# Who frees a stream buffer: TensorE's matmul in place of ScalarE's copy, four buffers of six blocks for three of five, and 12 row buffers for 16

## The chip, the cores and the metric

The kernel runs on one core of a Trainium2 chip. A core has five engines that run side by side and meet at semaphores: TensorE (PE in the profile; its weight loads are listed apart as PEld), VectorE (DVE), ScalarE (ACT), GpSimd (POOL) and SyncE (SP), which here does nothing but issue transfers. Sixteen DMA engines carry the transfers between HBM and the on-chip memory SBUF. SP's queue and GpSimd's queue of transfers are each worked off in order: a transfer whose condition is not met holds up those behind it. The metric is the device time of one execution in microseconds (us).

## The reference

A graph layer: every node's 128 features are normalized and clipped at zero, every edge sends its source's row through the 128 x 128 matrix of the edge's type, and every node adds up what arrives.

```python
h = jnp.maximum(_layernorm(x, axis=-1), 0.0)       # x: 12500 x 128
xs = h[src]                                         # 200000 edges
for i in range(4):                                  # edge types
    msgs = msgs + jnp.where((edge_type == i)[:, None], xs @ W[i] + b[i], 0.0)
out = x + segment_sum(msgs, dst, num_segments=12500)
```

The edges come sorted by `dst`, and `dst` is drawn as 12500 u^2 with u uniform, so that the first nodes get very many edges and the last few.

## The kernel before

**The table (the first 112 us).** Nodes are loaded in spans of three blocks (`load_span`, 33 spans; block j holds node 98 p + j on partition p). VectorE takes the statistics (L440), ScalarE normalizes (L461), and each value is split into three bf16 terms, which are stored to `htab` in HBM (L506, `third_part`), 768 bytes a node. The loaded spans lie in buffers of the pool `rows`, which has 16 buffers of 1536 bytes a partition. VectorE prepares in the same time the slots of the dense part. Here a planner that simulates the engines sets the order of all instructions.

**Two ways for the edges.** The 200000 edges are cut in 1563 chunks of 128. The first 512 chunks go to only 1392 nodes and are treated as dense; the other 1051 are gathered, in 64 groups of 16 chunks and four small ones at the end. The first three groups fetch rows of `x`; the other 1003 chunks fetch rows of `htab`.

- *Gathered part.* `gather` (L538) has GpSimd fetch a chunk's 128 source rows by an indirect transfer (L544), two chunks to a buffer `hm` of the same pool `rows`. While a group is worked on, the next one's gathers are in the program, and GpSimd issues them as buffers become free. `sum_up` (L569) multiplies each chunk with its one-hot matrix (L578, three matmuls a chunk), ScalarE copies the result (L581), `weigh` applies the four matrices (L605), and VectorE adds into a ring of destination columns (L666), which is turned and put out with `x` every 512 nodes (`leave`, `put_out`, L691, L696, L698; `fetch` loads the `x` rows at L677).

- *Dense part.* Its nodes are worked on in 18 batches of 27 units of three nodes (the first has 17). `count` (L940) makes for each unit the number of edges from every node and type, as a product of one-hots (VectorE makes them at L959 to L967, TensorE multiplies at L985, ScalarE copies the sum into `counts` at L991). `multiply` (L1024) then multiplies the counts with the whole table: for each of the 98 blocks, three matmuls (L1040) whose weights are the block's three terms and whose moving side is the batch's counts (324 columns), all added in one bank of PSUM.

**The stream.** The table does not stay in SBUF; each batch reads it anew. `hsp` is the pool of stream buffers `hs`; a buffer takes `HB` blocks, and SP loads it (L1032). There are `STREAM` = 3 buffers of `HB` = 5 blocks, so a batch has 20 refills (19 of five blocks, one of three). A refill has to wait until the buffer's former blocks have been read. The pool would make it wait for the last matmul that read them. But `held_by` adds a wait for the first of ScalarE's copies of counts (L991) that stands in the program behind that matmul (the list `left_at` holds the copies with the number of stream blocks read before them, `by_blocks`); this wait takes in the other. Only where no such copy stands there does a refill wait for TensorE itself.

**The order.** From the fourth group on the order on TensorE, VectorE and ScalarE is written out by hand: `dense_work` deals the steps of one batch's `multiply` and of the next one's `count` by their columns, `multiply` 0.15 of its length behind (`BEHIND`), so that a batch begins with some counting alone and ends with some multiplying alone; `pace` spreads this work evenly over the groups. SP and GpSimd follow the planner's order.

Of the kernel before, what the change touches and what calls it, by code (L numbers as in the profile page):

```python
# [55 lines left out]
C0 = 512  # L56
UB = 27
MANY = 16
HB = 5
SLOTS = 4  # L60
SETS = 4
STREAM = 3
BEHIND = 0.15
RING = 2048
OT = 4
# [9 lines left out]
def kernel(  # L75
# [10 lines left out]
    nc = tc.nc  # L86
    N, D = x.shape
    E = src.shape[0]
    NT, _, DO = w.shape
# [141 lines left out]
    flag = const.tile([P, 1], I32, name="flag")  # L231

    mid = ExitStack()
    hpool = mid.enter_context(tc.tile_pool(name="rows", bufs=16))
    opool = mid.enter_context(tc.tile_pool(name="onehots", bufs=2))
    spool = mid.enter_context(tc.tile_pool(name="typed", bufs=2))
    x_ps = mid.enter_context(tc.tile_pool(name="x_ps", bufs=4, space=PSUM))
# [279 lines left out]
    def held_by(one, by, reason):  # L517
        tc.add_manual_dep(
            one.ins,
            by.name,  # L520
            mybir.DependencyInfo(mybir.DependencyClass.Sync, mybir.DependencyReason.DATA),
            reason=reason,
        )
# [409 lines left out]
            nc.scalar.copy(acc[:, a:z], pn[:, : z - a])  # L933


    left_at = []
    by_blocks = [0]
    released = []

    def count(vs, counts):  # L940
        todo = []
        sets = []
        for i, u in enumerate(vs):
            of = slots_of(u)
            of = [(i, c, by, n == 0, n == len(of) - 1) for n, (c, by) in enumerate(of)]
            todo += of
            for one in [of[n : n + SLOTS] for n in range(0, len(of), SLOTS)]:
                if not sets or len(sets[-1]) + len(one) > SLOTS:
                    sets.append([])
                sets[-1] += one  # L950
        before = len(released)
        released.extend(None for _ in sets)

        def make(n):
            at = before + n
            o1 = op1.tile([P, SLOTS, P], BF16, name="o1")
            o2 = o2s[:, at % SETS]
            for k, (i, s, by, first, last) in enumerate(sets[n]):
                one = nc.vector.tensor_scalar(o2[:, k, :NB], iota_n, hkT[:, s : s + 1], None, ALU.is_equal)  # L959
                if k == 0 and at >= SETS:  # L960
                    held_by(one, released[at - SETS], "a set of slots has been counted as a whole")
                if by == 1.0:
                    one = nc.vector.tensor_scalar(o1[:, k], iota_1, loT[:, s : s + 1], None, ALU.is_equal)
                else:
                    if by is None:
                        by = byT[:, (s - PAIRS) // 2 : (s - PAIRS) // 2 + 1]
                    one = nc.vector.tensor_scalar(o1[:, k], iota_1, loT[:, s : s + 1], by, ALU.is_equal, ALU.mult)  # L967
                yield o1[:, k], o2[:, k], one.ins

        making = []  # L970
        made = []
        done = 0
        for n, of in enumerate(sets):
            while len(making) < min(n + 3, len(sets)):
                making.append(make(len(making)))
                made.append([])
            for m in range(n, min(n + 2, len(sets))):
                made[m] += list(making[m])
            for k, (i, s, by, first, last) in enumerate(of):
                if n + 2 < len(sets) and len(made[n + 2]) < len(sets[n + 2]):  # L980
                    made[n + 2].append(next(making[n + 2]))
                o1, o2, _ = made[n][k]
                if first:
                    pb = x_ps.tile([P, NB + NT], F32, name="pt")
                one = nc.tensor.matmul(pb, o1, o2, start=first, stop=last)  # L985
                if k == 0:
                    held_by(one, made[n][-1][2], "a set of slots is counted when all of it is made")
                if k == len(of) - 1:
                    released[before + n] = one.ins
                if last:  # L990
                    one = nc.scalar.copy(counts[:, :, i * NT : (i + 1) * NT], pb.rearrange("p (b t) -> p b t", t=NT))  # L991
                    left_at.append((by_blocks[0], one.ins))
                done += 1
                yield done / len(todo)
            made[n] = None

        def check_sums():
            n = len(vs)
            bi = sdp.tile([P, UB], I32, name="bi")
            nc.vector.tensor_copy(bi[:, :n], counts[:, NW, : n * NT].rearrange("p (i t) -> p i t", t=NT)[:, :, 0])  # L1000
            yield True
            bb = sdp.tile([P, 3, UB], I32, name="bb")
            nc.vector.tensor_single_scalar(bb[:, 0, :n], bi[:, :n], 255, op=ALU.bitwise_and)
            nc.vector.tensor_single_scalar(bb[:, 2, :n], bi[:, :n], 16, op=ALU.arith_shift_right)
            yield True
            nc.vector.tensor_single_scalar(bi[:, :n], bi[:, :n], 8, op=ALU.arith_shift_right)
            nc.vector.tensor_single_scalar(bb[:, 1, :n], bi[:, :n], 255, op=ALU.bitwise_and)
            yield True
            bf = sdp.tile([P, 3, UB], F32, name="bf")
            nc.vector.tensor_copy(bf[:, :, :n], bb[:, :, :n])  # L1010
            yield True
            top = sdp.tile([P, 2], F32, name="top")
            nc.vector.tensor_reduce(top[:, 0:1], bf[:, :, :n], AX.XY, ALU.max)
            nc.vector.tensor_reduce(top[:, 1:2], bf[:, :, :n], AX.XY, ALU.add)
            yield True
            nc.vector.tensor_max(most, most, top[:, 0:1])
            nc.vector.tensor_add(held, held, top[:, 1:2])

        checks.append(check_sums())
# [4 lines left out]
    def multiply(vs, counts):  # L1024
        nu = len(vs)

        counts = counts.bitcast(F8)
        pa = a_ps.tile([P, 512], F32, name="pa")
        for j0 in range(0, NW, HB):
            j1 = min(j0 + HB, NW)  # L1030
            hs = hsp.tile([P, HB, D3], BF16, name="hs")
            one = nc.sync.dma_start(hs[:, : j1 - j0, :], htab.rearrange("(p j) f -> p j f", j=NW)[:, j0:j1, :])  # L1032
            free = [by for n, by in left_at if n > by_blocks[0] - STREAM]
            if free and by_blocks[0] >= STREAM:
                held_by(one, free[0], "the buffer of the stream is free")
            del left_at[: len(left_at) - len(free)]
            for j in range(j0, j1):
                of = counts[:, j, : nu * NT * 4].rearrange("p (v m) -> p m v", m=4)[:, :3, :]
                for c in range(3):
                    nc.tensor.matmul(  # L1040
                        pa[:, : 3 * nu * NT].rearrange("p (m v) -> p m v", m=3),
                        hs[:, j - j0, c * D : (c + 1) * D],
                        of,
                        start=(j == 0 and c == 0),
                        stop=(j == NW - 1 and c == 2),
                    )
                if j + 1 == j1:
                    by_blocks[0] += 1
                if j + 1 < NW:
                    yield (j + 1) / NW  # L1050
        sd = sdp.tile([P, 3 * UB * NT], F32, name="sd")
        nc.scalar.activation(sd[:, : 3 * nu * NT], pa[:, : 3 * nu * NT], AF.Copy, scale=512.0)  # L1052
        def tail():
            py = x_ps.tile([P, 3 * UB], F32, name="pt")
            for t in range(NT):
                nc.tensor.matmul(  # L1056
                    py[:, : 3 * nu],
                    wsb[:, t, :],
                    sd[:, : 3 * nu * NT].rearrange("p (v t) -> p v t", t=NT)[:, :, t],
                    start=(t == 0),  # L1060
                    stop=(t == NT - 1),
                )

            def rest():
                for m in range(3):
                    i = 0
                    while i < nu:
                        if vs[i][m] is None:
                            i += 1
                            continue  # L1070
                        k, d = vs[i][m]
                        by = 2 if m < 2 and k == 0 and d >= PAIRS else 1
                        n = next((e for e in range(1, nu - i) if vs[i + e][m] != (k, d + e * by)), nu - i)
                        to = acc[:, d : d + (n - 1) * by + 1 : by]
                        nc.vector.tensor_tensor(to, to, py[:, m * nu + i : m * nu + i + n], ALU.add)
                        i += n

            tails.append(rest)

        tails.append(tail)  # L1080
        yield 1.0
# [448 lines left out]
```

## Time and profile before

| what | us |
|---|---|
| median of three runs | 1751.6 (1746.14 to 1752.2) |
| profiled execution, its own time | 1744.29 |
| its span, first to last instruction | 1742.5 |
| TensorE busy | 1435.4 |
| GpSimd busy | 1031.1 |
| VectorE busy | 1015.9 |
| ScalarE busy | 450.0 |
| mean granted TensorE clock | 0.926 |

The lines below come from that one execution. In a row of the waits stand the engine and line that waited, what ended the wait, the total in us, how often, and the longest. A group of instructions reads: line, engine, operation, tiles out<-in, shapes, count, then busy us and mean ns, then idle us of the engine before them and what ended it. "SPq" is SP's queue of transfers, "DMA hs<-htab" the landing of a refill, "issue" an idle time for which the profile shows no cause, "remote" one whose releaser is not in the trace. In a window's row stand, behind the stretch and its length, each engine's busy us with its count of instructions, the granted clock of TensorE (1.00 is full speed), the busy share of the DMA engines and GB/s. Some matmul records are missing from such a trace, and ends of matmuls are modelled.

### The profile page before, as it was taken

How to read it: one execution, taken by the hardware profiler on the slowest of the kernel's cores; microseconds unless marked ns; L12 is line 12 of the kernel's file. 1: busy time of each engine (PE TensorE's matmuls, PEld its weight loads, DVE VectorE, ACT ScalarE, POOL GpSimd, SP SyncE). 2: the span in 40 equal slices, each digit the busy share in tenths (PEclk: the TensorE clock that was granted, in tenths of full speed). 3: DMA queues.
4: the chain of work that ended last, by engine and by line, in shares of the span. 5: the costliest groups of instructions: out<-in, count | busy, mean ns of one | idle time of the engine just before them, and what ended most of it. 6: DMA issues, size and time to landing. Idle time of an engine off the chain costs nothing.

```text
span 1742.5 us, 32539 instructions
## 1 busy us (share of the span) xinstructions
PE 1435.4 (82%) x10984; PEld 938.3 (54%) x10984; DVE 1015.9 (58%) x5305; ACT 450.0 (26%) x1095; POOL 1031.1 (59%) x1078
## 2 busy tenths in 40 slices
PE   3876779787979787888888889888888989889875
PEld 1345565554656455555555555555555556555554
DVE  6972867565565556574647555756564556555334
ACT  5783322121212121212121222222222222122011
POOL 6536656565656565656665656666656566656561
PEclk8976799998999899999999999999999899999997
DMA  6542466565646465666555555655555655556652
GB/s 204 179 146 81 144 196 188 173 208 169 196 158 206 158 197 169 206 187 193 175 188 189 175 183 174 200 181 187 178 190 169 197 173 189 173 179 188 196 185 67
DMA packets 144538, 308.92 MB, mean 177 GB/s; under 512 B 26762, under 2 KB 77372, under 8 KB 144365
## 3 DMA queue, kind: packets, MB, share of 16 engines
q1 hardware_dynamic: 94685, 204.98, 35.9%
q0 software_dynamic: 49680, 101.81, 19.9%
q8 instruction: 86, 1.41, 0.3%
q14 instruction: 87, 0.71, 0.1%
HBM read 290.65 MB, written 16.04 MB: 176 GB/s over the span
## 4 chain that ended last, share of the span: by engine, by line
PE 52%; issue 19%; DMA 14%; DVE 5%; another core or an unknown queue 4%; ACT 4%; SPq 2%; DVEq 0%; ACTq 0%
PE pa L1040 27%; DMA hs<-htab 14%; PE pt L985 8%; PE py L605 5%; PE ps L578 4%; ACT counts L991 2%; PE pt L1056 2%; SPq L1032 1%; PE ps L635 1%; DVE oh L561 1%; PE py L596 1%; PE pt L691 1%; DVE o L967 1%; ACT sb L581 1%
## 5 line engine op out<-in xcount | busy, mean ns | idle before, releaser
L544 POOL DMA_INDIRECT hm<-htab,srcT x1003 | 974.6, 972 | 642.5 <-issue 227.1
L1040 PE MATMUL pa<-counts,hs 128*128 128x324 fp8e4 (+1 forms) x5292 | 970.4, 309 | 195.1 <-DMA hs<-htab 150.7
L1040 PEld LDWEIGHTS <-hs 128*128 128x128 bf16 x5292 | 490.9, 98 | 478.1 <-DMA hs<-htab 187.3
L959 DVE TENSOR_SCALAR o<-iota_n,hkT 128x392 bf16<-128x392 f16 x1167 | 381.3, 327 | 97.7 <-PE pt L985 44.1
L985 PE MATMUL pt<-o,o 128*128 128x396 bf16 x1167 | 374.9, 345 | 23.2 <-issue 10.4
L991 ACT CAST counts<-pt 128x396 int32<-128x396 f32 x476 | 230.0, 493 | 555.8 <-PE pt L985 306.3
L561 DVE TENSOR_SCALAR oh<-iota_b,keyT 128x56 bf16<-128x56 bf16 (+8 forms) x1003 | 171.5, 258 | 328.9 <-PE py L596 89.8
L581 ACT COPY sb<-ps 128x224 f32<-128x224 f32 (+8 forms) x251 | 99.7, 397 | 529.4 <-PE ps L578 237.5
L666 DVE TENSOR_TENSOR ring<-ring,py 128x14 f32 (+7 forms) x976 | 171.2, 175 | 82.5 <-PE py L605 20.8
L578 PEld LDWEIGHTS <-hm 128*128 128x128 bf16 x3009 | 166.1, 100 | 75.3 <-issue 30.1
L578 PE MATMUL ps<-oh,hm 128*128 128x56 bf16 (+8 forms) x3009 | 189.3, 199 | 18.0 <-issue 13.9
L967 DVE TENSOR_SCALAR o<-iota,loT 128x128 bf16<-128x128 bf16 x644 | 175.2, 272 | 0.0
L985 PEld LDWEIGHTS <-o 128*128 128x128 bf16 x1167 | 114.0, 99 | 77.3 <-issue 23.9
L967 DVE TENSOR_SCALAR o<-iota,loT,byT 128x128 bf16<-128x128 bf16 x417 | 139.6, 335 | 0.0
L605 PE MATMUL py<-sb,wsb 128*128 128x224 f32 (+7 forms) x488 | 130.3, 410 | 0.4 <-issue 0.3
L605 PEld LDWEIGHTS py<-sb,wsb 128*128 128x128 f32 x488 | 89.9, 197 | 24.6 <-issue 2.2
L528 POOL DMA_INDIRECT hx<-in_x_dram,srcT x48 | 50.9, 1060 | 34.1 <-issue 12.1
L1000 DVE COPY bi<-counts 128x27 int32<-128x27 int32 (+1 forms) x18 | 4.2, 232 | 106.0 <-issue 62.0
L600 ACT CAST cnt<-py 128x224 bf16<-128x224 f32 (+7 forms) x61 | 24.1, 395 | 112.4 <-PE py L596 35.2
L461 ACT ACTIVATE h<-hm,nmrt,rstdt 128x128 f32<-128x128 f32 x98 | 42.7, 492 | 2.2 <-DVE vart L446 1.9
L1056 PEld LDWEIGHTS pt<-sd,wsb 128*128 128x128 f32 x144 | 31.3, 304 | 6.9 <-ACT sd L1052 4.8
L1056 PE MATMUL pt<-sd,wsb 128*128 128x81 f32 (+1 forms) x144 | 31.0, 379 | 4.7 <-ACT sd L1052 4.7
(234 smaller groups left out, 639.6 us busy)
## 6 DMA issues: line engine op xcount, KB each, us to landing
hs<-htab SPq DMA_DIRECT2D x342, 480.0 KB
hm<-htab,srcT POOLq DMA_INDIRECT x1003
htab<-h SPq DMA_DIRECT2D x32, 288.0 KB
xo<-in_x_dram SPq DMA_DIRECT2D x23, 256.0 KB
out_dram<-xo SPq DMA_DIRECT2D x23, 256.0 KB
hs<-htab SPq DMA_DIRECT2D x18, 288.0 KB
hm<-in_x_dram SPq DMA_DIRECT2D x18, 192.0 KB
hm<-in_x_dram SPq DMA_DIRECT2D x14, 168.0 KB
```

The lines of the kernel that those rows point to most:

```text
L544: one = nc.gpsimd.indirect_dma_start(out=hm[:, (i - h0) * D3 : (i - h0 + 1) * D3], out_offset=None, in_=htab, in_offset=bass.IndirectOffse ...
L561: nc.vector.tensor_scalar(oh[:, i, :], iota_b[:, :K], keyf[:, at : at + 1], None, ALU.is_equal)
L578: nc.tensor.matmul(ps[:, i - i0, :], rows(i, c), oh[:, i, :], start=(c == 0), stop=(c == 2))
L581: nc.scalar.copy(sb[:, i0:i1].rearrange("p g t n -> p g (t n)"), ps[:, : i1 - i0, :])
L605: nc.tensor.matmul(py[:, :g, :], wsb[:, t, :], sb[:, :g, t, :], start=False, stop=(t == NT - 1))
L666: nc.vector.tensor_tensor(to, to, of(i), ALU.add)
L959: one = nc.vector.tensor_scalar(o2[:, k, :NB], iota_n, hkT[:, s : s + 1], None, ALU.is_equal)
L967: one = nc.vector.tensor_scalar(o1[:, k], iota_1, loT[:, s : s + 1], by, ALU.is_equal, ALU.mult)
L985: one = nc.tensor.matmul(pb, o1, o2, start=first, stop=last)
L991: one = nc.scalar.copy(counts[:, :, i * NT : (i + 1) * NT], pb.rearrange("p (b t) -> p b t", t=NT))
L1040: nc.tensor.matmul(pa[:, : 3 * nu * NT].rearrange("p (m v) -> p m v", m=3), hs[:, j - j0, c * D : (c + 1) * D], of, start=(j == 0 and c == 0),
L1056: nc.tensor.matmul(py[:, : 3 * nu], wsb[:, t, :], sd[:, : 3 * nu * NT].rearrange("p (v t) -> p v t", t=NT)[:, :, t], start=(t == 0), stop= ...
```

## The change

The list of ScalarE's copies and the extra wait on them are taken out: a refill of a stream buffer waits for the matmul that read the buffer last, and for nothing of ScalarE's. The stream gets four buffers of six blocks for three of five: a batch has 17 refills (16 of six blocks, one of two), each of 576 KB where it was 480 KB. The pool `rows`, from which both the loads of nodes and the gathered rows take their buffers, has 12 for 16. Per partition the stream grows from 11520 to 18432 bytes and the rows shrink from 24576 to 18432.

In the order as built, TensorE's matmuls, VectorE's one-hots and ScalarE's copies of the long stage stand as they did. In the first 112 us the planner gives another order on all engines but GpSimd, since loads of nodes wait for earlier buffers: load 12 is the first to wait for one, where load 16 was.

```diff
-HB = 5
+HB = 6
-STREAM = 3
+STREAM = 4
...
-    hpool = mid.enter_context(tc.tile_pool(name="rows", bufs=16))
+    hpool = mid.enter_context(tc.tile_pool(name="rows", bufs=12))
...
-    left_at = []
-    by_blocks = [0]
     released = []
...
                 if last:
-                    one = nc.scalar.copy(counts[:, :, i * NT : (i + 1) * NT], pb.rearrange("p (b t) -> p b t", t=NT))
-                    left_at.append((by_blocks[0], one.ins))
+                    nc.scalar.copy(counts[:, :, i * NT : (i + 1) * NT], pb.rearrange("p (b t) -> p b t", t=NT))
...
             hs = hsp.tile([P, HB, D3], BF16, name="hs")
-            one = nc.sync.dma_start(hs[:, : j1 - j0, :], htab.rearrange("(p j) f -> p j f", j=NW)[:, j0:j1, :])
-            free = [by for n, by in left_at if n > by_blocks[0] - STREAM]
-            if free and by_blocks[0] >= STREAM:
-                held_by(one, free[0], "the buffer of the stream is free")
-            del left_at[: len(left_at) - len(free)]
+            nc.sync.dma_start(hs[:, : j1 - j0, :], htab.rearrange("(p j) f -> p j f", j=NW)[:, j0:j1, :])
             for j in range(j0, j1):
...
-                if j + 1 == j1:
-                    by_blocks[0] += 1
                 if j + 1 < NW:
                     yield (j + 1) / NW
```

## The prediction

> **What bounds the kernel now.** I read the page's totals first, then the table of waits for the whole span, then the chain of waits around one of the stalls, then the timeline and short windows there.
>
> ```profile
> span 1742.5 us, 32539 instructions
> PE 1435.4 (82%) x10984; PEld 938.3 (54%) x10984; DVE 1015.9 (58%) x5305; ACT 450.0 (26%) x1095; POOL 1031.1 (59%) x1078
> ...
> L1040 PE MATMUL pa<-counts,hs 128*128 128x324 fp8e4 (+1 forms) x5292 | 970.4, 309 | 195.1 <-DMA hs<-htab 150.7
> ```
>
> ```profile
> SPq L1032 <- ACT counts L991: 633.3, 146, 12.1
> ```
>
> ```profile
> PEld L1040 <- DMA hs<-htab: 187.3, 106, 8.5
> PE pa L1040 <- DMA hs<-htab: 150.7, 88, 8.1
> ```
>
> TensorE is the busiest engine, and what it waits for in the long stage is one thing: the stream buffer `hs`. The queue of SP, which issues these transfers, stands 633 us in front of ScalarE's copies of counts. So the buffers are refilled late, and late because of the copy, not because of the transfer. One place shows it, in the chain (start, length, what):
>
> ```profile
> 822.39 0.32 SPq L1032
> 822.71 0.05 issue
> 822.76 0.02 SPq L1032
> 822.78 10.68 issue
> 833.45 3.34 DMA hs<-htab
> 836.80 0.05 issue
> 836.84 0.99 PE pa L1040 x3
> ```
>
> and in the timeline of the same stretch:
>
> ```profile
> 827.01 1.45 PE L1040 MATMUL pa<-counts,hs 128*128 128x324 fp8e4 x9
> ...
> 832.94 0.49 ACT L991 CAST counts<-pt 128x396 int32<-128x396 f32 x1 [0.16 <-remote]
> ...
> 836.84 0.99 PE L1040 MATMUL pa<-counts,hs 128*128 128x324 fp8e4 x3 [5.06 <-DMA hs<-htab]
> ```
>
> TensorE had read the last of the batch's buffers by 828.5. The next refill goes out at 833.45, when the first copy of the next batch's counts ends; it lands 3.34 us later, and TensorE has stood 5.06 us. This turn comes once per batch (18 batches); the other stalls are shorter ones of the same kind.
>
> The stall has a second price:
>
> ```profile
> core 0: us, PE busy (x) PEld busy (x) DVE busy (x) ACT busy (x) POOL busy (x), PEclk, DMA share, GB/s
> 190.00:1690.00 1500.00, 1278.01 (x10221) 845.74 (x10220) 869.01 (x4610) 330.51 (x786) 913.85 (x941) 0.95 0.58 185
> ...
> 829.60:833.00 3.40, 1.59 (x9) 0.48 (x8) 2.27 (x13) 0.78 (x3) 2.33 (x3) 1.00 0.28 79
> 833.00:836.40 3.40, 0.00 (x0) 0.00 (x0) 1.61 (x9) 0.43 (x1) 2.48 (x4) 0.50 0.70 207
> 836.40:839.90 3.50, 3.06 (x13) 2.27 (x14) 0.00 (x0) 0.00 (x0) 0.69 (x1) 0.51 0.84 332
> 839.90:843.30 3.40, 3.40 (x36) 2.27 (x36) 2.60 (x14) 1.04 (x3) 1.79 (x2) 1.00 0.12 32
> ```
>
> After a stretch of 3.4 us with TensorE 47% busy the granted clock halves, and it comes back only after a busy stretch: 13 matmuls in 3.5 us, then 36 in 3.4. Over the long stage the mean grant is 0.95.
>
> **The change part by part.**
>
> *Release by TensorE, four buffers of six.* A refill now waits for the last matmul that read its buffer. Between that matmul and the first that needs the refill stand three other buffers, 3 x 6 blocks x 3 = 54 matmuls, or 42 where one of them is the short buffer of two blocks that ends a batch.
>
> ```profile
> 783.36 0.59 PE L1040 MATMUL pa<-counts,hs 128*128 128x324 fp8e4 x3
> 783.80 0.33 PE L985 MATMUL pt<-o,o 128*128 128x396 bf16 x1
> 783.96 0.59 PE L1040 MATMUL pa<-counts,hs 128*128 128x324 fp8e4 x3
> ...
> 784.17 0.49 ACT L991 CAST counts<-pt 128x396 int32<-128x396 f32 x1
> ```
>
> ```profile
> hs<-htab SPq DMA_DIRECT2D x342, 480.0 KB
> ```
>
> Three of these matmuls take 783.80 - 783.36 = 0.44 us, so 54 take 8 us and 42 take 6.2 us, with no slot or row work between. Landing took 3.34 us for 480 KB; for 576 KB I estimate 3.34 x 1.2 = 4.0. Both spacings cover it, so I let all these stalls go. What they are worth: 150.7 us by the matmuls' row, 187.3 by the weight loads'. The loads' row starts while the last matmul still runs, one spacing of 0.15 us in each of 106 waits: 187.3 - 16 = 171 us. Taken: 171; the ends are kept. The refills drop from 20 to 17 a batch (98 blocks), with the same bytes.
>
> Queued behind SP's waits are not only refills:
>
> ```profile
> SPq L698 <- DVE xo L696: 41.8, 12, 9.5
> ```
>
> A refill behind such a wait is late by up to 9.5 us against 8 - 4 = 4 us to spare; the mean of 3.5 us is hidden, the longest would show some 5 us. Bound 0 to +10, in the 8 us below.
>
> *The clock.* A grant of 0.95 means (1 - 0.95) x 2 = 10% of 1500 us, 150 us, at half speed. TensorE is busy 85% of the stage, so up to 128 us of work runs at half speed and 64 us could come back; 0 is the other end. Of its 1500 - 1278 = 222 us idle the stream is 171, 77%; I take 77% of 64 = 49 us.
>
> The Trainium skill ("TensorE: Matmul & The Clock Gate", Part 1) says that an idle window of about 3.4 us halves the clock and a busy one restores it. The window above halved it with 47% busy, so this trace does not agree: it shows more loss than the rule says. By the rule as written that stall would have cost no clock, and the forecast would be the first rival's 1588.
>
> *TensorE's signals.* At most 306 buffers end in a matmul that has to signal SP. The matmul of 783.80 releases the copy of 784.17, and the next starts 0.16 us after it, no later than the 396 columns need: 0 us, and 0.03 us a signal would still be +9 us, the upper bound. The Trainium skill (same page, Part 3, "The cost: per-tile semaphore tail") puts 26 ns on each signal; that would be 306 x 0.026 = 8 us on top.
>
> *Rows, 12 buffers for 16.* A buffer holds two gathered chunks, so GpSimd runs 24 chunks ahead, not 32.
>
> ```profile
> L544 POOL DMA_INDIRECT hm<-htab,srcT x928 | 901.6, 972 | 579.5 <-issue 209.7 <-PE ps L578 186.7 <-PE pt L985 96.0
> ```
>
> ```profile
> POOL hm L544 <- issue: 212.2, 687, 0.6
> POOL hm L544 <- PE ps L578: 190.2, 107, 6.8
> ```
>
> A gather costs 0.97 us and 212.2 / 687 = 0.31 us before it, 1.28 us; a group of 16 takes 20.5 us. The rest of its idle time is waiting for buffers, that is, for TensorE. The stage of 1500 us has some 61 groups, 24.6 us each; with 171 + 49 us gone it is 21.0. GpSimd then has 0.5 us a group to spare where it had 4. With 24 chunks of lead, 31 us, a landing like the stream's 3 to 4 us hides. TensorE has no wait for `hm` among its waits today; I take 0, with 0 to +20 us if the margin fails in places.
>
> *The first 112 us.* The same pool takes the loads of nodes.
>
> ```profile
> L192 SPq DMA_DIRECT2D hm<-in_x_dram x15: 13/246/555, 26.8 to 76.2; - x15
> ```
>
> ```profile
> L440 DVE BATCH_NORM_STATS2 stt<-hm x98: 233/276/295, 5.0 to 88.2; 128x6 f32<-128x128 f32 x98
> L461 ACT ACTIVATE h<-hm,nmrt,rstdt x98: 477/492/519, 13.9 to 108.1; 128x128 f32<-128x128 f32 x98
> ```
>
> Load number u now waits for span u - 12, not u - 16, to be normalized. Normalizing goes at (108.1 - 13.9) / 33 = 2.9 us a span, so span 20 is done at about 13.9 + 21 x 2.9 = 75 us, and the last load (32) went out at 76.2, twelve before its statistics at 88.2. SP's stores of the table stand behind these waits, and the planner reorders VectorE's work here. Bound -6 to +6 (half of those twelve either way); 0 taken.
>
> *What is late next.* VectorE's one-hots:
>
> ```profile
> PE pt L985 <- DVE o L967: 7.6, 3, 4.1
> ```
>
> With TensorE not waiting elsewhere VectorE has less time to run ahead; as much again, +8 us, is charged for this and for SP's other waits together.
>
> *The end.* The last gather starts 33 us before the span's end:
>
> ```profile
> L544 POOL DMA_INDIRECT hm<-htab,srcT x1003: 941/949/2188, 114.2 to 1709.7; - x168
> ```
>
> The last 27 chunks need 27 x 1.28 = 35 us of GpSimd, and 24 may be ahead: 0, at most +5.
>
> **Sum.** The profiled execution took 1744.3 us (span 1742.5). 1744.3 - 171 - 49 + 8 = 1532. The median of the runs, 1751.6, stands 7 us above this execution, so 1539 is forecast for a median: 12% less.
>
> **Rivals.**
>
> *The half-speed stretches stay*, because other gaps halve the clock: 1744.3 - 171 + 8 + 7 = 1588. Against it: the window of 829.6 that led into one.
>
> *The gathers become the bound.*
>
> ```profile
> L578 PE MATMUL ps<-oh,hm x3009: 179/197/294, 149.8 to 1729.2; 128*128 128x56 bf16 x27, 128*128 128x80 bf16 x27, 128*128 128x48 bf16 x24, 128*128 128x64 bf16 x24
> ```
>
> 150 us lie before their use and 33 after the last; 24 of the 1003 are there by then, and 979 follow one another. At 1.28 us that is 150 + 1253 + 33 = 1436 us; it decides from (1532 - 183) / 979 = 1.38 us a gather. In the stage they now come every 1500 / 941 = 1.59 us, waits included. Halfway, 1.44: 183 + 1410 + 7 = 1600. For it: a margin of 0.5 us a group. Against: nothing in the trace slows a gather but TensorE.
>
> *The change does not do what it says*: the refills still go out late, held by SP's other waits, and a quarter of the gain comes: 1744.3 - 55 + 7 = 1696. Against: 41.8 us of such waits against 633.
>
> *Slower*: with 12 buffers TensorE comes to wait for its rows. Release, gather, landing and use is a ring of 24 chunks; it binds when one trip takes more than 24 x 1.59 = 38 us, against a landing of some 4 us and two gathers of 1.28. To lose by 0.5% it would have to eat the 212 + 9 us as well, 1.59 + 221 / 979 = 1.82 us a chunk, a trip of 44 us: 1761 or more. Nothing in the profile points there.
>
> **How the numbers follow.** Forecast 0.62 (own range 1500 to 1570: ends of the stall term, 64 us of clock, +20). Half-speed stays 0.15 and gathers bind 0.12, near 1588 and 1600, both reaching 1625. A quarter only 0.05; no change within 0.5% (9 us, about what a measurement of this kernel tells from none) 0.02; slower 0.04. Faster: 0.62 + 0.15 + 0.12 + 0.05 = 0.94. The lower end is 1744.3 - 187 - 64 - 6 + 7 = 1494, taken as 1490; to hold eight in ten with some over, the upper end takes in both of these: 1625.
>
> **What would show it.** Right: SP's wait for the copies gone and its wait for TensorE in its place, with the stream's row in TensorE's waits under 20 us; granted clock 0.98 or more in the long stage; GpSimd's wait for buffers down from 0.3 to some 0.05 us a gather. Wrong: a wait of TensorE for `hm`, or long gaps before L985 ended by VectorE, or refills that go out right after another DMA of SP's.

## The result, and the profile after

The changed kernel takes 1665.6 us in the median of four runs (1663.0 to 1668.0); the kernel before, run beside it, 1751.9 us. The ratio is 0.950 with a 95% interval of 0.945 to 0.955: a gain of 86 us, where 212 were forecast. 1665.6 lies outside the range of 1490 to 1625.

The stream's stall is gone all the same. From the page of the changed kernel (the stream's matmul is L1033 now, its refill L1029):

```profile
span 1661.2 us, 32454 instructions
PE 1417.4 (85%) x10984; PEld 921.7 (55%) x10984; DVE 1014.6 (61%) x5305; ACT 446.9 (27%) x1095; POOL 1030.6 (62%) x1078
...
L544 POOL DMA_INDIRECT hm<-htab,srcT x1003 | 975.0, 972 | 565.5 <-issue 230.9
L1033 PE MATMUL pa<-counts,hs 128*128 128x324 fp8e4 (+1 forms) x5292 | 963.3, 305 | 79.2 <-issue 69.7
```

and from its waits, the largest of SP's queue:

```profile
SPq L1029 <- PE ps L578: 371.9, 88, 10.1
SPq L1029 <- PE pt L983: 312.8, 79, 8.5
```

SP's queue no longer stands in front of ScalarE's copies (633.3 us before) but of TensorE, and no wait of TensorE for `hs` is left (150.7 us before). The clock is better too; in the stretch of the long stage:

```profile
190.00:1610.00 1420.00, 1260.59 (x10164) 826.53 (x10162) 860.09 (x4560) 325.87 (x781) 911.28 (x937) 0.98 0.61 194
```

The grant is 0.98 where it was 0.95. But TensorE is busy 1260.59 of 1420 us, 89% (85% before), and what it waits for now has no name:

```profile
PE pa L1033 <- issue: 69.7, 134, 3.8
PE ps L578 <- issue: 32.7, 56, 1.2
```

One such place, in the timeline of TensorE, then of ScalarE, then of GpSimd (start, length, what; in brackets the idle time before it):

```profile
776.56 0.34 PE L578 MATMUL ps<-oh,hm 128*128 128x64 bf16 x6
776.74 1.72 PE L1033 MATMUL pa<-counts,hs 128*128 128x324 fp8e4 x9
...
779.34 0.28 PE L578 MATMUL ps<-oh,hm 128*128 128x64 bf16 x4
780.07 0.23 PE L578 MATMUL ps<-oh,hm 128*128 128x64 bf16 x2 [0.45 <-issue]
...
783.12 0.59 PE L1033 MATMUL pa<-counts,hs 128*128 128x324 fp8e4 x3 [0.89 <-ACT sd L1043]
```

```profile
776.26 0.37 ACT L581 COPY sb<-ps 128x256 f32<-128x256 f32 x1 [4.56 <-remote]
782.36 0.37 ACT L581 COPY sb<-ps 128x256 f32<-128x256 f32 x1 [5.73 <-PE pt L983]
```

```profile
776.50 1.01 POOL L544 DMA_INDIRECT hm<-htab,srcT  x1 [1.23 <-remote]
777.81 1.24 POOL L544 DMA_INDIRECT hm<-htab,srcT  x1 [0.30 <-issue]
779.35 1.17 POOL L544 DMA_INDIRECT hm<-htab,srcT  x1 [0.30 <-issue]
780.83 0.95 POOL L544 DMA_INDIRECT hm<-htab,srcT  x1 [0.30 <-issue]
782.59 0.94 POOL L544 DMA_INDIRECT hm<-htab,srcT  x1 [0.82 <-PE pt L983]
```

Three things are to be seen. TensorE stops for 0.45 us between the fourth and the fifth of six matmuls on one buffer, where it can have nothing to wait for. The six matmuls at 776.56 end a bank of four chunks, and ScalarE, idle, copies that bank at 782.36, 5.5 us after their record ends. And GpSimd issues four gathers 1.3 to 1.5 us apart, then stands 0.8 us (1.2 us before the first of them) until TensorE's signal comes, within 0.25 us of the start of ScalarE's copy. Counted over the stage from 230 to 1590 us, the copy of four chunks starts 3.35 us in the middle after the record of their last matmul begins (2.13 us in the kernel before, by the same count). TensorE's semaphore updates come in bunches: about half, some 660 of 1297, fall in the some 120 us in which GpSimd has been idle for more than 0.75 us; in such a bunch they follow each other by 0.08 us in the middle, though the matmuls that gave them lie further apart.

By place, with the groups counted from 0, so that group 3 is the first that fetches rows of `htab`: from the start of group 5 to that of group 62 a group takes 24.25 us (25.51 before, 21.0 forecast), 71.5 us less over 57 groups. Group 5 begins 13.6 us earlier, group 3 0.5 later; from group 62 on the kernel takes 3.8 us longer. Together 81.3 us, the difference of the two spans.

### The profile page after: what moved, and what is told of

It reads as the page before. It is cut to its first block, busy times and chain, and to the rows that moved or that the text cites. A ratio compares the mean times of both kernels' runs of the same rounds, so it can differ in the third digit from the quotient of the medians.

```text
span 1661.2 us, 32454 instructions
## 1 busy us (share of the span) xinstructions
PE 1417.4 (85%) x10984; PEld 921.7 (55%) x10984; DVE 1014.6 (61%) x5305; ACT 446.9 (27%) x1095; POOL 1030.6 (62%) x1078
## 4 chain that ended last, share of the span: by engine, by line
PE 74%; DVE 11%; issue 9%; another core or an unknown queue 2%; ACT 1%; DMA 1%; POOL 0%; SPq 0%; DVEq 0%; ACTq 0%; POOLq 0%
PE pa L1033 43%; PE pt L983 11%; PE ps L578 6%; PE py L605 6%; DVE o L957 2%; DVE o L965 2%; PE pt L1047 1%; DVE ring L666 1%; DVE oh L561 1%; PE ps L635 1%; PE py L596 1%; PE pt L691 1%; DVE stt L440 1%; POOL hm L544 0%
## 5 line engine op out<-in xcount | busy, mean ns | idle before, releaser
L544 POOL DMA_INDIRECT hm<-htab,srcT x1003 | 975.0, 972 | 565.5 <-issue 230.9
L1033 PE MATMUL pa<-counts,hs 128*128 128x324 fp8e4 (+1 forms) x5292 | 963.3, 305 | 79.2 <-issue 69.7
L1033 PEld LDWEIGHTS <-hs 128*128 128x128 bf16 x5292 | 492.3, 97 | 353.9 <-issue 132.7
L983 PE MATMUL pt<-o,o 128*128 128x396 bf16 x1167 | 369.5, 337 | 40.3 <-DVE o L965 21.4
L965 DVE TENSOR_SCALAR o<-iota,loT 128x128 bf16<-128x128 bf16 x644 | 177.2, 275 | 0.0
L983 PEld LDWEIGHTS <-o 128*128 128x128 bf16 x1167 | 111.3, 98 | 98.9 <-issue 30.2
L965 DVE TENSOR_SCALAR o<-iota,loT,byT 128x128 bf16<-128x128 bf16 x417 | 142.0, 340 | 0.0
L605 PEld LDWEIGHTS py<-sb,wsb 128*128 128x128 f32 x488 | 86.4, 190 | 32.9 <-issue 11.7
L490 PE MATMUL ps<-h,ident 128*128 128x384 f32 (+1 forms) x34 | 17.2, 591 | 15.7 <-issue 11.4
L596 PE MATMUL py<-oh,three 128*32 128x224 bf16 (+7 forms) x244 | 21.2, 311 | 7.6 <-issue 3.9
```

Source lines behind the costliest of these rows:

```text
L544: one = nc.gpsimd.indirect_dma_start(out=hm[:, (i - h0) * D3 : (i - h0 + 1) * D3], out_offset=None, in_=htab, in_offset=bass.IndirectOffse ...
L605: nc.tensor.matmul(py[:, :g, :], wsb[:, t, :], sb[:, :g, t, :], start=False, stop=(t == NT - 1))
L1033: nc.tensor.matmul(pa[:, : 3 * nu * NT].rearrange("p (m v) -> p m v", m=3), hs[:, j - j0, c * D : (c + 1) * D], of, start=(j == 0 and c == 0),
```

## Experiments

The theory formed from this trace: while GpSimd issues gathers, TensorE's signals leave late ("held signals"); consumers and GpSimd itself wait, TensorE's queue fills (its records never run more than some 31 matmuls ahead of a signal that is still out), and the groups take the length of GpSimd's cycle. The rivals: TensorE's own work is longer than the spacing of its records tells; the traffic holds it up; GpSimd's lead of 24 chunks is too short. The kernels ran on several chips, each beside the kernel before on the same chip, and ratios are to that; between chips the ratios are compared, since the kernel before does not take the same time on each.

**No gathers.** Same bytes, buffers and waits:

```diff
-                one = nc.gpsimd.indirect_dma_start(out=hm[...], in_=htab, in_offset=...)
+                j = (t0 + i) % (N // P)
+                one = nc.sync.dma_start(hm[:, (i - h0) * D3 : (i - h0 + 1) * D3], htab[j * P : (j + 1) * P, :])
```

> Built from the changed kernel (1665.6 us). Each of the 1003 gathers of 128 rows of htab by GpSimd is replaced by a plain transfer of 128 consecutive rows of htab on SP's queue: the same bytes into the same 12 buffers, the same waits, but GpSimd makes no descriptors in the long stage; the gathered part of the result is not the reference's. Three theories for the gain that is missing (24.2 us a group of 16 chunks where 21.0 was forecast). Held signals: while GpSimd issues gathers, TensorE's signals leave late (the copy of four finished chunks starts 3.3 us in the middle after its last matmul's record), TensorE's queue of some 31 matmuls fills and it stops at places where it has nothing to wait for; without the gathers the groups fall to about 21 us, 59 groups x 3.1 = 180 us less, about 1480 us. TensorE's own work: the matmuls take longer than the spacing of their records tells, the records run ahead and the pauses are that queue; no change, 1650 to 1680. Traffic: 186 GB/s of transfers hold up the reading of weights; the bytes are the same, so no change, 1650 to 1680. A buffer lead of 12 that is too short would also leave it at 1650 to 1680.

Measured: 1425.4 us, 0.815 of the kernel before (0.812 to 0.818), 240 us under the changed kernel. On its page:

```profile
L1029 PE MATMUL pa<-counts,hs 128*128 128x324 fp8e4 (+1 forms) x5292 | 927.1, 301 | 0.5 <-ACT sd L1039 0.5
L1029 PEld LDWEIGHTS <-hs 128*128 128x128 bf16 x5292 | 490.8, 96 | 230.1 <-issue 0.7
```

The same 5292 matmuls have 0.5 us of idle time before them for 79.2, the groups take 20.56 us, and a copy follows its last matmul's start by 0.24 us. Traffic is higher (217 GB/s over the span for 186). So TensorE's own work, traffic and lead fall as the cause; what is left is something that comes with GpSimd's gathers.

**More and fewer signals of TensorE.** Three sizes of the same stream room, and rows in larger buffers:

```diff
-HB = 6            # eight_of_three: 3        three_of_eight: 8
-STREAM = 4        # eight_of_three: 8        three_of_eight: 3
```

```diff
+HR = 4            # four_rows: gathered rows in 6 buffers of four chunks
-    hpool = mid.enter_context(tc.tile_pool(name="rows", bufs=12))
+    hpool = mid.enter_context(tc.tile_pool(name="rows", bufs=6))
```

> The changed kernel with the stream in eight buffers of three blocks instead of four of six: the same bytes and the same room, but TensorE signals 594 freed stream buffers instead of 306 and SP issues twice as many refills of half the size. Held signals: each signal of TensorE has a price while GpSimd gathers; spread over all, 0.8 us lost per four chunks over about 6.9 signals is 0.12 us each, 284 more signals are +33 us, about 1700; if a signal costs as much as the 0.72 us in which queued signals are seen to follow each other, up to +200. TensorE's own work and traffic: no change, 1655 to 1675.

> The changed kernel with the stream in three buffers of eight blocks: the same room, 72 signals of TensorE fewer, refills of 768 KB. Eight buffers of three gave 284 signals more and 10 us more (0.036 us a signal): by that price 3 us less, within the measurement, 1655 to 1670. If a refill of 768 KB comes too late with two buffers ahead, waits for hs come back and it is slower, 1680 to 1700.

> The changed kernel with rows in 6 buffers of four chunks instead of 12 of two: the same room, but TensorE frees a buffer of rows once in four chunks, at the matmul that ends the bank as well, so it gives 256 signals fewer. Held signals: 256 x 0.12 = 30 us less, about 1635, if the number of signals sets the price; no change if the cycle is pinned by GpSimd's four gathers (4 x 1.25 us) and one pause of about 1 us after them, which stays once in four chunks. TensorE's own work and traffic: no change, 1655 to 1680; a lead that is too short: slower, since rows come free later, 1680 to 1720.

Measured: eight of three 1675.8 us, 0.958 (0.953 to 0.963), 10 us over the changed kernel in time and 15 us by the ratios, with the intervals overlapping; three of eight 1692.0, 0.955 (0.951 to 0.958), on a chip where the kernel before takes 1772.8; four rows 1711.8, 0.977 (0.973 to 0.981). The number of signals is not the lever: 284 more cost some 0.04 to 0.05 us each, if anything, and fewer gained nothing. (The Trainium skill, "TensorE: Matmul & The Clock Gate", Part 3, has some 26 ns for each semaphore increment at the end of a group of packed matmuls; an estimate from that is 7 us for 284. The matmuls that free a stream buffer are not packed, and the measurement is too coarse to tell 7 us from nothing or from 15.) Four rows is not a clean test: its node loads have six buffers for twelve, so group 3 starts 19 us later, and only 0.50 us a group, 28 us, belongs to the long stage. There GpSimd, released once in four chunks, pauses 1.3 us in the mean for 1.0.

**The two parts of the change, each alone.**

```diff
 # release_only: TensorE frees the buffers, sizes as before
 HB = 5
 STREAM = 3
 hpool = mid.enter_context(tc.tile_pool(name="rows", bufs=16))
```

```diff
 # by_scalar: sizes of the change, held_by(one, free[0], ...) as before
 HB = 6
 STREAM = 4
 hpool = mid.enter_context(tc.tile_pool(name="rows", bufs=12))
```

> The release of the change without its sizes: TensorE's own matmuls free the stream's buffers, three buffers of five blocks and 16 buffers of rows as before. If the release is what took the stream's waits away and the rest is the cycle of gathers: about 1665 to 1690. If the release does little without the larger stream, since TensorE's signals leave late too (3.3 us in the middle): 1700 to 1750, with waits for hs left in the multiply's row.

> The sizes of the change without its release: four buffers of six blocks and 12 buffers of rows, the refills waiting for ScalarE's copies as before. TensorE gives 231 signals fewer than in the changed kernel. If the larger stream alone took the waits away: held signals forecasts 231 x 0.12 = 28 us under the changed kernel, about 1640, up to 100 us under it; TensorE's own work and traffic forecast about the changed kernel's time, 1655 to 1680. If the release by copies is what made the stream late, the stream's waits stay and it lies near the kernel before, 1720 to 1750.

Measured: the release alone 1701.9 us, 0.960 (0.956 to 0.964), on the chip of 1772.8; the sizes alone 1727.9, 0.988 (0.984 to 0.991), on one of 1748.3; the product is 0.948, the whole change 0.950, so the parts add up. Applied to the 1751.9 us of the first chip, the ratio of the release alone gives 1682 us, inside the first of its two forecasts; as a time, on the slower chip, it lies just inside the second. In TensorE's waits 18.7 us for `hs` are left with the release alone, and 64.1 with the sizes alone:

```profile
PE pa L1033 <- DMA hs<-htab: 18.7, 24, 2.0
```

```profile
PE pa L1040 <- DMA hs<-htab: 64.1, 17, 6.4
```

The forecast of 1640 for the sizes alone was made for the case that they take the stream's waits away; they do not, and for the case that the waits stay the forecast was 1720 to 1750, so this run says nothing on the price of signals. Group 5 starts at 214.1 us with the release alone and at 199.3 with the sizes alone (210.5 before, 196.9 after): the start's gain belongs to the sizes. Which of them, the larger stream or the fewer row buffers, this pair does not tell.

**Sixteen row buffers again.**

```diff
-HB = 6
+HB = 4
-    hpool = mid.enter_context(tc.tile_pool(name="rows", bufs=12))
+    hpool = mid.enter_context(tc.tile_pool(name="rows", bufs=16))
```

> The changed kernel with 16 buffers of rows again, paid for by a stream of four buffers of four blocks instead of six. If GpSimd's lead of 24 chunks instead of 32 were what keeps the groups at 24.2 us, they get shorter, about 1620. Held signals: GpSimd runs into the same wait eight chunks later, and the cycle stays as it is; 1660 to 1690, the upper end if 12 blocks ahead do not cover a refill.

Measured: 1701.3 us, 0.961 (0.957 to 0.964), on the chip of 1772.8; groups of 24.72 us. The release alone has 24.77 on that chip, and three of eight 24.76: with 12 buffers or 16, and with a stream of 15, 16 or 24 blocks, the group is as long. The lead is not what makes it so.

**Half of the gathers, and seven in eight.** Buffers of rows with `h0 // HG % 2` (or `% 8 == 7`) filled by the plain transfer of the first experiment:

```diff
+                if h0 // HG % 2:
+                    one = nc.sync.dma_start(hm[...], htab[j * P : (j + 1) * P, :])
+                else:
                     one = nc.gpsimd.indirect_dma_start(...)
```

> The changed kernel with every second buffer of rows (two chunks of each four) filled by plain transfers of consecutive rows on SP's queue, the others gathered by GpSimd as before: the same bytes, 502 gathers for 1003; half of the gathered part is not the reference's. The run with no gathers took 1425 us, 240 us less than the changed kernel. Held signals, with a cycle of GpSimd's gathers in a row and a pause: GpSimd has 2.5 us of gathers in about 5 us of four chunks, so TensorE's signals get out in its idle time and nearly all of the 240 us is gone, 1425 to 1455. A fixed price per gather (240 / 1003 = 0.24 us, as for contention by each gather): 502 x 0.24 = 120 us stay, about 1545.

Measured: 1427.6 us, 0.806 (0.803 to 0.809), again on the chip of 1772.8; groups of 20.58 us: with half the gathers nothing of the loss is left. It has no fixed price per gather.

> The changed kernel with one buffer of rows in eight (two chunks of each group of 16) filled by a plain transfer of consecutive rows; those chunks of the result are not the reference's. The cycle: 14 gathers of 1.25 us and 3.5 pauses of 0.95 us make 20.8 us a group, next to TensorE's 20.5 (5.13 us for four chunks in the run without gathers): 1440 to 1500. A price per gather: 240 us x 7/8 stay, about 1635.

This run, the next two and their first repetitions met a chip of another kind, on which the kernel before takes 1527 us with all its gathers. One gather in eight replaced: 1416.0 us, 0.927.

**Less work for TensorE**, and **the kernel before without gathers**:

```diff
-                for c in range(3):
+                for c in range(2):
...
-                        stop=(j == NW - 1 and c == 2),
+                        stop=(j == NW - 1 and c == 1),
```

> The changed kernel with two of the stream's three products for each block (the third term of the table is read but not multiplied, so the dense part of the result lacks it): 1764 matmuls of 0.144 us fewer, 254 us of TensorE's work, while the gathers stay as they are. If the groups' length is set by GpSimd's cycle (four gathers of 1.25 us in a row, then about 1 us in which TensorE's held signals come out), the time falls little: 1600 to 1650, or to 1540 if TensorE gets far enough ahead that six gathers run between pauses (8.45 us for six chunks). If TensorE's own work sets it: about 1410.

> The kernel before with all gathers replaced by plain transfers, as in the first run of this study (1425 us for the changed kernel): what the change is worth where GpSimd makes no descriptors. If the stream's waits before came from the release by copies and the small stream alone, as the prediction had it, they stay and the kernel lies 212 us above the changed one: about 1640. If the copies came late because TensorE's signals did (2.1 us in the middle in the kernel before), most of the waits go with the gathers: 1440 to 1520.

Measured on that chip: two terms 1412.7 us, 0.925; the kernel before without gathers 1520.7, 0.998 (0.995 to 1.001) of the same kernel with them. So on this chip the gathers cost next to nothing, and the first run cannot tell a cycle from TensorE's work. The changed kernel itself was measured next, on the same chip as it turned out, with the three again.

> The changed kernel itself, beside the kernel before on one more chip. On the chip of the last runs the kernel before takes 1527 us, as long as without gathers (1521), and the copies follow the last matmul of four chunks by 0.24 us; on the two chips before that it takes 1748 and 1773. If the hold of TensorE's signals by gathers belongs to the chip, this kernel takes 1415 to 1430 where the kernel before takes about 1527 (its time with one gather in eight replaced was 1416), and 1660 to 1690 where the kernel before takes about 1750. If it does not belong to the chip: 1660 to 1690 on each.

> Two of the stream's three products again (254 us of TensorE's work fewer). It took 1413 us on the chip where the kernel before takes 1527. On a chip that holds the signals (kernel before at about 1750): 1600 to 1650 if the cycle of four gathers and a pause sets the length of the groups, to 1540 if six gathers run between pauses; about 1410 if TensorE's work sets it. On a chip that does not: 1413 again.

> One buffer of rows in eight by a plain transfer again. On a chip that holds the signals: 1440 to 1500 by the cycle (20.8 us a group), about 1635 by a price per gather of 0.24 us. On a chip that does not: 1416 again.

> The kernel before without gathers again, 1521 us on the chip where the kernel before with them takes 1527. On a chip that holds the signals it should take the same, about 1520, since nothing holds them then: the kernel before loses some 230 us to its gathers there, the changed kernel 240, and the change is worth about 95 us with gathers or without.

Measured, the kernel before at 1527.9 us: the changed kernel 1419.4, 0.929 (0.924 to 0.933); two terms 1412.9; one in eight 1416.1; before without gathers 1520.5, 0.996 (0.992 to 0.999). The changed kernel, instruction for instruction the same, has on this chip:

```profile
span 1416.5 us, 32454 instructions
PE 1346.1 (95%) x10984; PEld 914.7 (65%) x10984; DVE 1013.3 (72%) x5305; ACT 459.5 (32%) x1095; POOL 1033.3 (73%) x1078
...
L544 POOL DMA_INDIRECT hm<-htab,srcT x1003 | 978.4, 975 | 341.7 <-issue 227.9
L1033 PE MATMUL pa<-counts,hs 128*128 128x324 fp8e4 (+1 forms) x5292 | 927.9, 302 | 0.5 <-ACT sd L1043 0.5
```

in its timeline of TensorE and of ScalarE:

```profile
644.25 0.34 PE L578 MATMUL ps<-oh,hm 128*128 128x64 bf16 x6
```

```profile
644.63 0.37 ACT L581 COPY sb<-ps 128x256 f32<-128x256 f32 x1 [2.55 <-PE ps L578]
```

The copy starts 0.04 us after the last matmul's end, here while GpSimd's gathers follow one another every 1.29 us with hardly a pause (5 over 0.35 us in 909). The groups take 20.66 us. Gathers do not hold TensorE's signals everywhere: the hold goes with the chip. Why, no run shows, and since most chips were met only once, anything else that differed from one meeting to the next is not excluded. The kernel before took 1748, 1773, 1750 and 1752 us on four of the chips used in this study and 1527 and 1525 on two.

What was left was the question of cycle or work on a chip that holds.

> Two of the stream's three products once more, for a chip that holds TensorE's signals (there the kernel before takes about 1750): 254 us of TensorE's work fewer with the same gathers. A cycle of four gathers (5.0 us) and a pause of about 1 us that sets the length of four chunks: 1600 to 1650; 1540 if six gathers run between pauses. TensorE's work stretched by late signals in proportion: about 1410 to 1450. If it meets a chip that does not hold them, 1413 as before, and nothing is told apart.

This run was on the second of the chips that do not hold: 1413.9 us.

> The same kernel with two of the stream's three products, once more for a chip that holds TensorE's signals (kernel before at about 1750): 1600 to 1650 (or to 1540) if a cycle of four gathers and a pause sets the length of four chunks, 1410 to 1450 if TensorE's work does. On a chip that does not hold them: 1413, and the question stays open.

This one held: 1651.6 us, 0.944 (0.939 to 0.948; the kernel before at 1750.4), groups of 24.06 us.

```profile
PE 1283.2 (78%) x9220; PEld 793.4 (48%) x9220; DVE 1017.9 (62%) x5305; ACT 445.2 (27%) x1095; POOL 1029.9 (62%) x1078
...
L544 POOL DMA_INDIRECT hm<-htab,srcT x1003 | 974.3, 971 | 554.4 <-issue 240.2
L1033 PE MATMUL pa<-counts,hs 128*128 128x324 fp8e4 (+1 forms) x3528 | 755.9, 320 | 107.0 <-issue 94.3
```

A third of the stream's matmuls gone, 254 us of work, and the time falls by 14 us: TensorE's work does not set the length there. GpSimd's idle time is what it was (554.4 for 565.5 us). Six gathers in a row became common (some 75 of its 180 pauses follow six, some 90 follow four), but the pauses grew with them, from 1.0 to 1.1 us in the mean, so the 1540 us of that case did not come.

> One buffer of rows in eight by a plain transfer, for a chip that holds TensorE's signals (kernel before at about 1750; there two of three products took 1652 and no gathers 1425). A cycle of gathers and pauses: 14 gathers of 1.25 us and 3.5 pauses of 0.95 us a group, 20.8 us next to TensorE's 20.5: 1440 to 1500. A price per gather of 0.24 us: about 1635. On a chip that does not hold them: 1416 again, and it stays open.

It held too: 1533.1 us, 0.877 (0.873 to 0.880; the kernel before at 1752.4). The forecast of 1440 to 1500 missed, and so did the price per gather. The cycle comes near it if there is one pause for each four chunks and not for each four gathers, a reading made after the run: 3.5 gathers of 1.25 us and the changed kernel's pause of 1.06 make 5.44 us for four chunks; 5.53 were measured (groups of 22.11 us). The same sum is 5.0 + 1.06 = 6.06 for the changed kernel and 5.0 + 1.01 = 6.01 with two terms; with half of the gathers it is 2.5 + 1.1 = 3.6, and TensorE's own 5.14 (20.56 us a group without gathers) set the length (5.14 measured). The pause in these sums is what is left of the measured length; that it comes out at 1.0 to 1.15 us for three kernels, with 3.5 or 4 gathers and with 254 us more or less of TensorE's work, is what speaks for the cycle. The pauses themselves, those that exceed the usual 0.30 us before a gather by 0.35 us or more, are 1.0 us over it in the mean in the changed kernel and 1.1 in the other two.

No version that computes the whole layer was faster than the changed kernel.

## Why the prediction was wrong

*What bounds the kernel.* Half right. TensorE did wait for late refills, and late because of the copies. What was not seen is why the copies were so late. Where nothing is held, the kernel before, here without its gathers, has

```profile
PE pa L1036 <- DMA hs<-htab: 83.1, 54, 3.4
```

```profile
SPq L1028 <- ACT counts L987: 147.1, 186, 4.4
```

for 150.7 and 633.3 us. Nearly half of the stall term was the hold, reaching TensorE by way of ScalarE. The trace of before had it in sight, in ScalarE's timeline beside the row of TensorE at 780.21 and in GpSimd's:

```profile
780.21 0.34 PE L578 MATMUL ps<-oh,hm 128*128 128x64 bf16 x6
```

```profile
783.90 0.37 ACT L581 COPY sb<-ps 128x256 f32<-128x256 f32 x1 [1.73 <-PE ps L578]
```

```profile
784.13 0.95 POOL L544 DMA_INDIRECT hm<-htab,srcT  x1 [1.26 <-PE ps L578]
...
790.10 0.97 POOL L544 DMA_INDIRECT hm<-htab,srcT  x1 [1.25 <-PE pt L985]
```

ScalarE is idle for 1.73 us while the matmuls it waits for have ended, by their record, 3.35 us earlier, and GpSimd's pauses come 5.97 us apart, about the 6.06 us that four chunks then take in the changed kernel.

The prediction's own rows had it too. "The matmul of 783.80 releases the copy of 784.17" is a misreading, and on it the signals were put at nothing. By the order of the program, with all 1167 matmuls of L985 and all 476 copies in the trace, the copy of 784.17 takes the product of 781.41, 2.4 us after the end of that record, and the matmul of 783.80 is copied at 785.49, 1.4 us after its end:

```profile
781.41 0.33 PE L985 MATMUL pt<-o,o 128*128 128x396 bf16 x1
```

```profile
785.49 0.49 ACT L991 CAST counts<-pt 128x396 int32<-128x396 f32 x1 [0.83 <-PE pt L985]
```

The copy of 832.94, behind which the refill of the stall shown in the prediction went out, comes 2.05 us after its matmul's record ends. From 230 to 1590 us these copies start 1.37 us in the middle after the end of their matmul's record in the kernel before, 2.62 in the changed kernel, and 0.04 in the changed kernel on the chip that does not hold.

*The stall term, -171 us.* This is the step that failed, by its size. Every one of these waits went, as forecast, and 86 us came, since the time under them was not TensorE's to have: "the rest of its idle time is waiting for buffers, that is, for TensorE" and "with 171 + 49 us gone it is 21.0" took the group to be as short as TensorE can make it. On a chip that holds, four chunks take 6.06 us, and still 6.01 with a third of the stream's matmuls taken away; the kernel before, at 6.38, stood 0.32 us above that, and 0.32 us for each four chunks is what the long stage gained. Where nothing is held the same way of reckoning is good: the stalls of the kernel before without gathers are 105.3 us by the loads' row, less one spacing in each of 72, 94 us, and the change brings 108 us there with gathers (1527.9 to 1419.4). Without gathers it brings 95 (1520.5, against 1425.4 in the first experiment, on another chip). The groups are 20.66 us, next to the 21.0 of the prediction.

*The clock, -49 us.* The grant rose from 0.95 to 0.98 as the sign said, but a faster TensorE was worth nothing in that cycle. Two terms show it: their mean grant is 0.894 for 0.958, and they are not slower. That the half-speed stretches stay, the first rival, did not happen. One step beside this term was wrong: by the rule that the prediction quotes from the Trainium skill ("TensorE: Matmul & The Clock Gate", Part 1), the stall shown would have cost the same clock. It holds a stretch that is idle as a whole (833.00 to 836.40, PE 0.00 us), so by that rule too the clock is halved for the matmuls from 836.84 on, and the 1588 us do not follow from it. What the trace does show is the halving at 833.0, one stretch earlier, after a stretch 47% busy.

*TensorE's signals, 0 to +9 us.* 284 more signals cost 10 us by the times (1675.8 against 1665.6) and 15 by the ratios, if anything, 0.04 to 0.05 us each where the upper bound had 0.03. Beside the 126 us that are missing, the number of signals was right to leave out. That a signal can be 3 us late was not thought of, since the rows of 783.80 and 784.17 were read as a signal in time.

*Rows, 0.* Right: 16 buffers brought nothing back, and TensorE waits for `hm` twice, 2.3 us together.

*The first 112 us, 0.* Right: group 3 starts at 150.3 for 149.8. The 13.6 us by which group 5 starts earlier were not in the sum as a term of their own.

*What is late next, +8 us.* VectorE's one-hots, 7.6 us before, are 21.4 us now (the wait of L983 for L965), 14 more. *The end, 0 to +5:* 3.8.

*The rivals.* "The gathers become the bound" is the one that comes nearest, with a chance of 0.12, and its rule was right: it decides from 1.38 us a gather, and the gathers come every 1.516 us in the stage. What slows them it did not name: a gather itself is no longer than before, and the pauses make the difference. Its own sum at that pace, 183 + 979 x 1.516 + 7 = 1674 us, is 8 us from the measured time; the pace is the one measured afterwards, so only the form of the sum is borne out. What spoke against it, "nothing in the trace slows a gather but TensorE", was the misreading: the pause before each fourth gather was booked on TensorE because TensorE's signal ended it. The price of 1600, halfway between two rows, was too low.

*The signs.* SP's wait, the stream's row and the clock came out as named. GpSimd's wait for buffers did not: by the same count as in the prediction it is 1.516 - 1.28 = 0.24 us a gather, where 0.31 was before and 0.05 the sign of a right forecast. Of the wrong signs that were named (waits for `hm`, VectorE, SP's other transfers) none came to more than the 21.4 us of VectorE; the one that came, pauses between matmuls with no releaser, was not on the list, though the kernel before has 40 us of it.

## What to carry to other kernels

A wait that an engine's signal ends is not the same as a wait for that engine's work: compare the end of the producer's record with the start of its consumer, and where an idle consumer starts microseconds later, count the cycle that is really closed (here four gathers and a pause) before a stall is booked as gain. The time under a stall belongs to the next longest cycle, and that can be a chain of hand-overs in which no engine is busy. Where GpSimd gathers without a break beside TensorE, measure on more than one chip: leaving it half idle took the whole loss away, and one gather in eight fewer took about half.

## What the runs showed of the hardware

- On four chips TensorE's signals came late while GpSimd issued indirect gathers back to back: in the changed kernel 3.35 us in the middle from the start of a matmul's record to the copy that waits for it, against 0.24 us without gathers on a chip that holds and 0.24 us with gathers on one that does not. Signals that queue while gathers run follow each other in steps of about 0.72 us (or come together); once GpSimd has been idle for some 0.75 us, 0.08 us apart.
- What is late is the signal: up to six come in a bunch, less than 0.15 us from one to the next, from matmuls whose records lie up to microseconds apart. Whether the matmuls themselves wait as well cannot be told from the records.
- The loss is large, 224 us of 1752 in the kernel before and 246 of 1666 in the changed one, and goes with the chip: on two chips the same program shows next to none of it. What differs there is open. It wasn't tried whether another way to issue gathers avoids the hold.
- With nothing held, taking 254 us of work from TensorE gave only 6 us (1419.4 to 1412.9): the gathers, every 1.28 us, are the next bound there, as the second rival had it. TensorE now waits for the rows, which it does not in the changed kernel on that chip. The rival's sum is 183 + 979 x 1.28 = 1436, less 13 for that chip's shorter first stage (group 3 starts at 137.9 us for 150.3): 1423, 10 us over the measured time.

```profile
PE ps L578 <- DMA hm<-htab,srcT: 167.9, 186, 3.2
```
